# Mixture-of-experts block: the last five expert tiles on one set of sums, the other set loaded meanwhile

## The chip, the cores and the metric

One core of a Trainium2 chip runs the whole program in one launch. The metric is device time in microseconds (us) from start to end, as the median of several runs. A profile of one further run shows every instruction with its engine, its start and its length. The engines are TensorE (PE in the profile; its weight loads are PEld), VectorE (DVE), ScalarE (ACT), GpSimd (POOL) and SyncE (SP). SP issues most transfers; POOL issues the indirect ones. Sixteen DMA engines move the data.

## The reference, cut to what matters

An attention layer is followed by a layer of 16 experts, and each of the two is added to its input and normalised. The second half is what the change concerns:

```python
x = _layernorm(x + attention(x))               # 4 x 1024 tokens of 256 numbers
raw_gate = softmax(einsum('btd,de->bte', x, gate))
_, topk_idx = top_k(raw_gate, 3)               # three experts for a token
gate_topk = normalised(mask * raw_gate)
hidden = relu(einsum('btd,edh->bteh', x, W1) + b1)
expert_out = einsum('bteh,ehd->bted', hidden, W2) + b2
x = _layernorm(x + einsum('bte,bted->btd', gate_topk, expert_out))
```

All numbers are 32-bit floats.

## The kernel before

**Up to the experts.** Attention comes first; its last matmuls with the values (L479) start at 1120.7 us, the first of the experts at 1129.0 us. A router then chooses three experts for each token and writes the token's row, with its number and its gates, to a table in DRAM (`xs`), sorted by expert. Two arrays in DRAM, `sums[0]` and `sums[1]`, collect the output, one row of 256 numbers for each of the 4096 tokens. Before the experts run, `sums[0]` receives the tokens themselves (the residual) and `sums[1]` zeros.

**The tiles of the experts.** The function `moe` works through 56 tiles, t = 0 to 55 (`NUSUAL` is 56), and through some more in a branch (`tc.If`) that this input doesn't take. A full tile has 256 rows of one expert, a short one 128. In the last 32 tiles, three full ones are followed by one short one, so 51 and 55 are short and 52, 53 and 54 are full. A tile passes these steps:

- `load`: SP fetches the rows and the expert's weights (about 1.15 MB), four tiles ahead;
- `turn`: TensorE transposes the rows, VectorE copies them out (`xg`) and derives row numbers (`ids`) and gates;
- `hidden`: 16 matmuls, then four relus on ScalarE (`hid`, L1099);
- `expert_out`: 16 matmuls (8 for a short tile), then VectorE adds the bias (`y`, L1115), multiplies by the gates, one instruction for each 128 rows (L1121), and POOL issues one scatter for each 128 rows (L1125).

A scatter is an indirect DMA that adds 128 rows of 1 KB to rows of one of the two arrays of sums. The two scatters of a full tile are declared independent of each other, since a token occurs once in an expert's list; for those of different tiles nothing is declared. The set is chosen by the tile's parity (`sums_of`, L1010), so neighbours add to different sets. POOL's scatters are kept in program order (`behind`, L1014).

The orders of TensorE and SP are written out by hand in `run` (L1185). In turn t it has `turn(t+1)`, `hidden(t)`, `expert_out(t-1)`, but at the last turn `expert_out(54)` comes ahead of `hidden(55)`.

**The end.** After the tiles, `fetch` (L1217) loads both sets in nine pieces on SP's queue, `res` from `sums[0]` and `more` from `sums[1]`: seven pieces of four rows of 256 numbers for each of 128 partitions (512 KB from each set), and two pieces of two rows (256 KB). For each piece, `statistics` adds `more` to `res` on POOL (L1226), takes mean and variance on VectorE (L1230, L1232) and a root on ScalarE (L1234). `scale`, one piece behind, takes a reciprocal (L1241) and an offset (L1243) on VectorE, scales on ScalarE (L1245) and stores on SP (L1249). The orders of VectorE, ScalarE and SP are those of the program here.

Of the kernel before, what the change touches and what calls it, by code (L numbers as in the profile page):

```python
# [29 lines left out]
FP = mybir.dt.float32  # L30
# [5 lines left out]
SYNC = mybir.DependencyInfo(mybir.DependencyClass.Sync, mybir.DependencyReason.DATA)  # L36
NO_SYNC = mybir.DependencyInfo(mybir.DependencyClass.NoSync, mybir.DependencyReason.DATA)

P = 128
B, T, D = 4, 1024, 256  # L40
# [8 lines left out]
FC = FF // P  # L49
NTC = NT // P  # L50
# [16 lines left out]
NUSUAL = NL1 + NL2 + NHUSUAL  # L67
# [904 lines left out]
def moe(tc, router, first, late_rows, last_norm, acc, ident, eps_t, wall, xs, sums, out):  # L972
    nc = tc.nc
    with ExitStack() as ctx:
        def pool(name, bufs, **kw):
            return ctx.enter_context(
                tc.tile_pool(name=name, bufs=bufs, reuse_waits="tile", **kw)
            )
# [7 lines left out]
        op = pool("m_out", 1)  # L986
# [4 lines left out]
        ps_r = pool("ps_r", 1, space=PSUM)  # L991

        wall_v = wall.rearrange("(e p) r -> e p r", p=P)
        st = {}
        lists = [first, None, None, None]
        order = [(0, i) for i in range(NL0)] + [(1, i) for i in range(NL1 - NL0)]
        n_first = NL2 - 3 * NHUSUAL
# [5 lines left out]
        def of(t):  # L1003
            k, i = order[t]
            return lists[k], i

        def halves(t):
            return 1 if order[t][0] == 3 else SH

        def sums_of(t):  # L1010

            return sums[t % 2]

        def behind(i):  # L1014

            tc.add_manual_dep(i.ins, router.behind.ins.name, NO_SYNC, reason="issue order")
            router.behind = i
            return i
# [33 lines left out]
        def turn(t):  # L1052
            (_, _, rank), i = of(t)
            x, nh = st[t][0], halves(t)
            ps = ps_t.tile([P, DC, S], FP, tag="t")
            for c in range(DC):
                for h in range(nh):
                    nc.tensor.transpose(ps[:, c, ts(h, P)], x[:, h, ts(c, P)], ident)  # L1058
            xg = xgp.tile([P, DC, S], FP, tag="xg")
            with in_turn(t < NUSUAL):  # L1060
                st["turned"] = nc.vector.tensor_copy(xg[:, :, : nh * P], ps[:, :, : nh * P])  # L1061
            with tc.issue_after(st["turned"].ins):
                small(t, xg, ps)

        def in_turn(usual=True):
            return tc.issue_after(router.on_dve.ins) if usual else nullcontext()

        def small(t, xg, ps):
            (_, _, rank), i = of(t)
            x, nh = st[t][0], halves(t)  # L1070
            ids = gp.tile([P, SH], I32, tag="ids", name="ids")
            nc.vector.tensor_copy(ids[:, :nh], x[:, :nh, ID])
            mine = gp.tile([P, SH, TOPK], FP, tag="mine", name="mine")
            nc.vector.tensor_scalar(
                mine[:, :nh], x[:, :nh, RK : RK + TOPK], rank[:, i : i + 1], 1.0,
                ALU.is_equal, ALU.mult,
            )
            nc.vector.tensor_tensor(
                mine[:, :nh], mine[:, :nh], x[:, :nh, GT : GT + TOPK], ALU.mult
            )  # L1080
            gates = gp.tile([P, SH], FP, tag="gates", name="gates")
            nc.vector.tensor_reduce(gates[:, :nh], mine[:, :nh], AX.X, ALU.add)
            st[t] += [xg, ids, gates]

        def hidden(t):
            _, w, xg, _, _ = st[t]
            n = halves(t) * P
            hid = hp.tile([P, FC, S], FP, tag="hid")
            per = 512 // n
            for f0 in range(0, FC, per):  # L1090
                ps = ps_h.tile([P, per, n], FP, tag="h")
                for f in range(f0, f0 + per):
                    for c in range(DC):
                        nc.tensor.matmul(  # L1094
                            ps[:, f - f0, :], lhsT=w[:, ds(c * FF + f * P, P)], rhs=xg[:, c, :n],
                            start=(c == 0), stop=(c == DC - 1),
                        )
                for f in range(f0, f0 + per):
                    nc.scalar.activation(  # L1099
                        hid[:, f, :n], ps[:, f - f0, :], AF.Relu, bias=w[:, ds(B1_AT + f, 1)]  # L1100
                    )
            st[t].append(hid)

        def expert_out(t):
            _, w, _, ids, gates, hid = st.pop(t)
            nh = halves(t)
            ps = ps_o.tile([P, SH, D], FP, tag="o")
            for h in range(nh):
                for f in range(FC):
                    nc.tensor.matmul(  # L1110
                        ps[:, h, :], lhsT=hid[:, f, ts(h, P)], rhs=w[:, ds(W2_AT + f * D, D)],
                        start=(f == 0), stop=(f == FC - 1),
                    )
            y = yp.tile([P, SH, D], FP, tag="y")
            nc.vector.tensor_tensor(  # L1115
                y[:, :nh], ps[:, :nh],
                w[:, ds(B2_AT, D)].unsqueeze(1).to_broadcast([P, nh, D]), ALU.add,
            )
            before = None
            for h in range(nh):  # L1120
                router.on_dve = nc.vector.tensor_scalar(  # L1121
                    y[:, h, :], y[:, h, :], gates[:, h : h + 1], 1.0, ALU.mult, ALU.mult
                )
            for h in range(nh):
                s = behind(nc.gpsimd.indirect_dma_start(  # L1125
                    out=sums_of(t), out_offset=bass.IndirectOffsetOnAxis(ap=ids[:, h : h + 1], axis=0),
                    in_=y[:, h, :], in_offset=None, compute_op=ALU.add,
                ))
                if before is not None:
                    tc.declare_no_dep(  # L1130
                        s.ins, before.ins, reason="an expert has a token once: other rows"
                    )
                before = s
                if late_rows:
                    rows_of_last_but_one(3)
                elif spread_rows and t >= 5:
                    spread_rows.pop(0)()
# [15 lines left out]
        def rows_of_last_but_one(k, wait=False):  # L1153
            for _ in range(min(k, len(late_rows))):
                i = late_rows.pop(0)()
                if wait:
                    tc.add_manual_dep(
                        i.ins, st["turned"].ins.name, SYNC, reason="apart from the rows before"
                    )
# [19 lines left out]

        sums_v = [s[:NT].rearrange("(p c) d -> p c d", p=P) for s in sums]  # L1180
        out_v = out.rearrange("b t d -> (b t) d").rearrange("(p c) d -> p c d", p=P)
        rows = [(c, 4) for c in range(0, NTC - 4, 4)] + [(NTC - 4, 2), (NTC - 2, 2)]
        n_k = len(rows)

        def run(t0, t1, begun=lambda: None):  # L1185
            with tc.manual_schedule(engines={mybir.EngineType.PE, mybir.EngineType.SP}):
                for t in range(t0, t0 + 4):
                    load(t)
                turn(t0)
                begun()  # L1190
                for t in range(t0, t1):
                    if t + 4 < t1:
                        load(t + 4)
                    if t + 1 < t1:
                        turn(t + 1)
                    if t == t1 - 1:
                        expert_out(t - 1)
                    hidden(t)

                    for go in side.get(t, []):  # L1200
                        go()
                    if t0 < t < t1 - 1:
                        expert_out(t - 1)
                expert_out(t1 - 1)
# [3 lines left out]


        run(0, NUSUAL, lambda: last_norm(sp))  # L1210
        used = nc.values_load(router.used[0:1, 0:1], min_val=0, max_val=NHALF)
        with tc.If(used > NHUSUAL):
            run(NUSUAL, len(order))

        res, more = [], []

        def fetch(k):  # L1217
            c, m = rows[k]
            for of_set, got, name in ((0, res, "res"), (1, more, "more")):
                t = op.tile([P, m, D], FP, tag=f"{name}{k}", name=name)  # L1220
                nc.sync.dma_start(out=t, in_=sums_v[of_set][:, ds(c, m), :])
                got.append(t)

        def statistics(k):
            r, m = res[k], rows[k][1]
# [26 lines left out]
        with tc.manual_schedule(engines={ENG.DVE, ENG.Activation, ENG.SP}):  # L1252
            for k in range(n_k):
                fetch(k)
            for k in range(n_k):
                statistics(k)
                if k > 0:
                    scale(k - 1)
            scale(n_k - 1)
# [112 lines left out]
```

## Time and profile before

| | us |
|---|---|
| median of three runs | 1561.87 |
| lowest and highest run | 1559.64, 1563.41 |
| the profiled execution | 1561.28 |
| its span, first to last instruction | 1559.5 |
| mean granted TensorE clock, share of full | 0.985 |
| TensorE matmul busy | 1499.4 (96%) |
| last matmul ends | about 1518.5 |
| first load of the end is issued | 1523.36 |
| first add of the end | 1528.80 |

Times inside the run are us from the start of the span. A timeline row gives the start, the length, the engine, the line of the kernel, the operation, what it writes and reads, the shape and the count; a bracket tells how long the engine had been idle and what ended that. "issue" there means that the profile shows no other instruction as the cause. SPq marks what SP only hands to the DMA engines. A landing is the time from the start of an instruction that issues a DMA to the last byte's arrival.

### The profile page before, as it was taken

The page shows a single profiled execution, that of the slowest core. Times are in us where ns is not written, and L with a number is a line of the kernel's source. Part 1 is how long each engine was busy: PE and PEld are TensorE (multiplying, and loading weights), DVE is VectorE, ACT ScalarE, POOL GpSimd, SP SyncE. Part 2 cuts the span into 40 slices and gives each one's busy share as a digit, 9 for nine tenths or more (in the row PEclk, how much of TensorE's full clock was granted, in tenths as well). Part 3 has the DMA queues.
Part 4 walks back from the last instruction along what each step waited for, and adds up shares of the span by engine and source line. Part 5 has one row for each costly group of instructions (what it writes and reads, how often), then busy time and mean ns, then how long its engine had stood idle before and what let it go on. Part 6 is the DMA issues. An engine that isn't in the chain of part 4 may idle for free.

```text
span 1559.5 us, 52512 instructions
## 1 busy us (share of the span) xinstructions
PE 1499.4 (96%) x20844; PEld 1049.4 (67%) x20844; DVE 1174.7 (75%) x3679; ACT 729.6 (47%) x1693; POOL 979.6 (63%) x932
## 2 busy tenths in 40 slices
PE   8999999999999999999999999999899999999990
PEld 5566666666666666666666666665688888888880
DVE  5788888898899999878999999889857333333335
ACT  4555555557455555665555556645342222222224
POOL 3676565776556567776776667767457764444445
PEclk9999999999999999999999999999999999999995
DMA  6464545545454554564556445645488998888858
GB/s 203 128 166 123 142 117 150 152 134 176 116 143 116 149 152 119 151 191 136 150 145 171 117 129 139 192 125 137 160 311 266 373 297 226 257 257 259 258 130 329
DMA packets 120473, 280.34 MB, mean 180 GB/s; under 512 B 21392, under 2 KB 64656, under 8 KB 108688
## 3 DMA queue, kind: packets, MB, share of 16 engines
q1 hardware_dynamic: 100304, 250.05, 53.0%
q0 software_dynamic: 19584, 26.62, 8.1%
q8 instruction: 166, 2.72, 0.7%
q14 instruction: 83, 0.68, 0.1%
q10 hardware_dynamic: 336, 0.27, 0.1%
HBM read 186.81 MB, written 61.09 MB: 159 GB/s over the span
## 4 chain that ended last, share of the span: by engine, by line
PE 88%; DVE 7%; issue 2%; DMA 2%; ACT 1%; POOL 0%; SPq 0%; ACTq 0%; DVEq 0%; POOLq 0%
PE y_ps L479 18%; PE s L393 17%; PE pp L290 14%; PE ps L1110 11%; PE ps L1094 11%; PE oo L508 8%; PE vv L343 7%; PE ps L1058 1%; DVE p L401 1%; DVE t_first L452 1%; PE lg_ps L727 1%; DMA vr<-v_d 1%; DVE o_stats L1230 1%; PE x_ps L719 0%; DVE t_last L452 0%
## 5 line engine op out<-in xcount | busy, mean ns | idle before, releaser
L433 POOL TENSOR_SCALAR p<-p,rinv 128x512 f32<-128x512 f32 (+7 forms) x512 | 374.7, 747 | 336.1 <-DVE rinv L430 307.2
L416 ACT ACTIVATE p<-p,nmax 128x512 f32<-128x512 f32 (+7 forms) x512 | 391.7, 766 | 407.3 <-DVE nmax L401 318.8
L393 PE MATMUL s<-rotk,rotq 64*128 64x512 f32 (+3 forms) x1536 | 310.9, 513 | 3.3 <-DVE rotk L326 1.6
L452 DVE STREAM_TRANSPOSE t_first<-p 128x512 f32<-128x512 f32 (+3 forms) x512 | 275.8, 581 | 7.4 <-PE y_ps L479 7.3
L1125 POOL DMA_INDIRECT sums<-y,ids x104 | 163.1, 1568 | 162.2 <-DVE y L1121 128.7
L290 PE MATMUL pp<-xT,wqk 128*128 128x512 f32 x512 | 249.9, 612 | 3.4 <-DVE nmax L401 3.3
L1099 ACT ACTIVATE hid<-ps,w 128x256 f32<-128x256 f32 (+1 forms) x224 | 89.6, 455 | 289.9 <-issue 237.7
L479 PE MATMUL y_ps<-t_first,vr 32*64 32x224 f32 (+3 forms) x8192 | 206.2, 332 | 5.6 <-DVE t_first L452 2.2
L393 PEld LDWEIGHTS s<-rotk,rotq 64*128 64x128 f32 x1536 | 138.7, 186 | 100.1 <-issue 53.2
L479 PEld LDWEIGHTS y_ps<-t_first,vr 32*64 32x64 f32 x8192 | 166.9, 132 | 53.7 <-issue 45.9
L1115 DVE TENSOR_TENSOR y<-ps,w 128x512 f32<-128x512 f32 (+1 forms) x56 | 36.5, 652 | 216.7 <-PE ps L1110 184.9
L1094 PE MATMUL ps<-xg,w 128*128 128x256 f32 (+1 forms) x896 | 189.5, 365 | 1.4 <-DVE xg L1061 0.7
L1110 PE MATMUL ps<-w,hid 128*128 128x256 f32 x832 | 188.8, 379 | 0.5 <-ACT hid L1099 0.5
L401 DVE CUSTOM_DVE_ANT_0 p<-s,zero_and_mask,nmax 128x512 f32<-128x512 f32 x256 | 181.7, 747 | 2.9 <-PE s L393 0.7
L401 DVE CUSTOM_DVE_ANT_0 p<-s,mask 128x512 f32<-128x512 f32 (+1 forms) x256 | 131.8, 551 | 60.3 <-PE s L393 59.9
L1110 PEld LDWEIGHTS ps<-w,hid 128*128 128x128 f32 x832 | 157.2, 190 | 21.5 <-ACT hid L1099 0.7
L1094 PEld LDWEIGHTS ps<-xg,w 128*128 128x128 f32 x896 | 157.3, 190 | 19.1 <-DVE xg L1061 1.0
L290 PEld LDWEIGHTS pp<-xT,wqk 128*128 128x128 f32 x512 | 89.5, 189 | 119.7 <-issue 62.4
L479 PEld LDWEIGHTS y_ps<-t_last,vr 32*64 32x64 f32 x7424 | 105.2, 131 | 76.5 <-issue 49.8
L508 PE MATMUL oo<-wo,yT 128*128 128x256 f32 x512 | 141.0, 398 | 2.3 <-DVE yT L495 1.1
L479 PE MATMUL y_ps<-t_last,vr 32*64 32x32 f32 (+3 forms) x7424 | 127.1, 243 | 0.5 <-DVE t_last L452 0.4
L824 POOL DMA_INDIRECT xs<-acc,slots x96 | 97.3, 1013 | 44.0 <-issue 21.5
(191 smaller groups left out, 1835.1 us busy)
## 6 DMA issues: line engine op xcount, KB each, us to landing
w<-in_wall_dram SPq DMA_DIRECT2D x56, 1154.0 KB
vr<-v_d SPq DMA_DIRECT2D x256, 128.0 KB
vr<-v_d SPq DMA_DIRECT2D x128, 256.0 KB
swq<-rawq SPq DMA_DIRECT2D x256, 64.0 KB
v_d<-v SPq DMA_DIRECT2D x128, 128.0 KB
swk<-rawk SPq DMA_DIRECT2D x124, 128.0 KB
x<-xs SPq DMA_DIRECT2D x48, 264.0 KB
wqk<-in_w_qk_dram SPq DMA_DIRECT2D x32, 256.0 KB
```

The lines of the kernel that those rows point to most:

```text
L290: nc.tensor.matmul(ps, lhsT=wqk[n][:, c, i, :], rhs=xts[b, g][:, c, :], start=(c == 0), stop=(c == DC - 1),)
L343: nc.tensor.matmul(ps[:, u, :], lhsT=xts[b, cc // 2][:, c, ts(cc % 2 * 2 + u, P)], rhs=wv[n][:, c, :], start=(c == 0), stop=(c == DC - 1),)
L393: nc.tensor.matmul(s[:, :n_k], lhsT=rot[n, 0, qc // 4][ts(hh, KD), ts(qc % 4, P)], rhs=k[ts(hh, KD), ds(k0, n_k)], start=True, stop=True,)
L401: i = nc.vector.tensor_tensor_reduce(out=probs[n, qc, hh][:, ds(k0, n_k)], in0=s[:, :n_k], in1=masks[qc % 2][:, 512 - n_k :] if diag else ...
L416: order["exp"] = nc.scalar.activation(pr, pr, AF.Exp, bias=m, scale=-1.0, accum_out=rsum[:, hh : hh + 1])
L433: order["divide"] = router.behind = nc.gpsimd.tensor_scalar(pr, pr, rinv[:, hh : hh + 1], 1.0, ALU.mult, ALU.mult)
L452: order["turn"] = router.on_dve = after(nc.vector.transpose(turned[n][h][:, hh, :, ds(i - 4 * h, n_j, step=7 - 4 * h), :], probs[n, i, hh] ...
L479: nc.tensor.matmul(st[n][a][ts(hh, KD), ds(32 * (j + skip), 32 * (TC - j - skip))], lhsT=v[ts(a, 32), c * 8 + 2 * u + jh % 2, ts(hh, KD)], ...
L508: nc.tensor.matmul(ps[:, v, :], lhsT=st[n][:, ts(2 * h + v, P)], rhs=wo[n], start=True, stop=True,)
L1094: nc.tensor.matmul(ps[:, f - f0, :], lhsT=w[:, ds(c * FF + f * P, P)], rhs=xg[:, c, :n], start=(c == 0), stop=(c == DC - 1),)
L1110: nc.tensor.matmul(ps[:, h, :], lhsT=hid[:, f, ts(h, P)], rhs=w[:, ds(W2_AT + f * D, D)], start=(f == 0), stop=(f == FC - 1),)
L1125: s = behind(nc.gpsimd.indirect_dma_start(out=sums_of(t), out_offset=bass.IndirectOffsetOnAxis(ap=ids[:, h : h + 1], axis=0), in_=y[:, h, ...
```

## The change

- Tiles 51 to 55 all add to `sums[1]`.
- While tiles 53 to 55 run, SP loads all of `sums[0]` into `res`. These loads, `first_sums`, are now ten, the first piece being split into two of two rows, and most wait for a mark: a certain relu, bias addition or gate multiplication of a tile.
- The last two turns are written out in `last_two` (z is 55): tile 55 passes `hidden` ahead of tile 54, and `expert_out` too.
- After the tiles only `more` is loaded, in the same ten pieces.
- In the branch that isn't taken here, `res` is loaded again at the end.

```diff
         def sums_of(t):
-            return sums[t % 2]
+            return sums[1 if NUSUAL - 5 <= t < NUSUAL else t % 2]
...
-                    nc.scalar.activation(
+                    marks["hid", t, f] = nc.scalar.activation(
...
-            nc.vector.tensor_tensor(
+            marks["y", t] = nc.vector.tensor_tensor(
...
+            marks["scaled", t] = router.on_dve
...
-        rows = [(c, 4) for c in range(0, NTC - 4, 4)] + [(NTC - 4, 2), (NTC - 2, 2)]
+        rows = [(0, 2), (2, 2)] + [(c, 4) for c in range(4, NTC - 4, 4)] + [(NTC - 4, 2), (NTC - 2, 2)]
         n_k = len(rows)
+        res = [op.tile([P, m, D], FP, tag=f"res{k}", name="res") for k, (_, m) in enumerate(rows)]
+
+        def first_sums(k, *mark):
+            c, m = rows[k]
+            d = nc.sync.dma_start(out=res[k], in_=sums_v[0][:, ds(c, m), :])
+            if mark:
+                tc.add_manual_dep(d.ins, marks[mark].ins.name, SYNC, reason="one after another")
+
+        def last_two(z):
+            first_sums(0, "hid", z - 2, FC - 1)
+            first_sums(1)
+            first_sums(2, "y", z - 3)
+            turn(z)
+            first_sums(3, "scaled", z - 3)
+            expert_out(z - 2)
+            first_sums(4, "y", z - 2)
+            first_sums(5, "scaled", z - 2)
+            hidden(z)
+            first_sums(6, "hid", z, FC - 1)
+            hidden(z - 1)
+            first_sums(7, "hid", z - 1, FC // 2 - 1)
+            first_sums(8, "hid", z - 1, FC - 1)
+            first_sums(9)
+            expert_out(z)
+            expert_out(z - 1)
...
                 for t in range(t0, t1):
+                    if t == NUSUAL - 2:
+                        last_two(t + 1)
+                        return
                     if t + 4 < t1:
...
             run(NUSUAL, len(order))
-        res, more = [], []
+            for k in range(n_k):
+                first_sums(k)
+
+        more = []
 
         def fetch(k):
             c, m = rows[k]
-            for of_set, got, name in ((0, res, "res"), (1, more, "more")):
-                t = op.tile([P, m, D], FP, tag=f"{name}{k}", name=name)
-                nc.sync.dma_start(out=t, in_=sums_v[of_set][:, ds(c, m), :])
-                got.append(t)
+            t = op.tile([P, m, D], FP, tag=f"more{k}", name="more")
+            nc.sync.dma_start(out=t, in_=sums_v[1][:, ds(c, m), :])
+            more.append(t)
```

More of the change, by code (lines that the diff above doesn't have):

```diff
@@ L993, in moe @@
         wall_v = wall.rearrange("(e p) r -> e p r", p=P)
-        st = {}
+        st, marks = {}, {}
         lists = [first, None, None, None]
```

## The prediction

> **What bounds the kernel now.** I read four views in this order: the chain of waits from 1440 us on, the timeline of GpSimd (POOL) around the last tiles, the timelines after 1523 us, and the landing times of scatters, by windows that hold one or a few. t numbers the tiles, 0 to 55; the short last one is 55. E is the time at which the last scatter has landed.
>
> The chain of waits (start, duration, what):
>
> ```profile
> 1507.30 6.92 PE ps L1110 x32
> ...
> 1515.86 1.55 POOL sums L1125
> ...
> 1517.72 5.57 DMA sums<-y,ids
> ...
> 1524.87 6.70 DMA more<-sums
> ```
>
> TensorE is the chain up to 1514.2 us. After that it is the scatters, then the first loads of the two sets, then the last norm. The change touches only the end, so the sum is made there.
>
> The scatters of t=52 (second half), 53 (second half), 54 and 55, from the POOL timeline:
>
> ```profile
> 1506.88 1.55 POOL L1125 DMA_INDIRECT sums<-y,ids  x1 [0.30 <-issue]
> ...
> 1514.01 1.55 POOL L1125 DMA_INDIRECT sums<-y,ids  x1 [0.30 <-issue]
> ...
> 1517.72 1.55 POOL L1125 DMA_INDIRECT sums<-y,ids  x1 [0.30 <-issue]
> 1519.64 1.55 POOL L1125 DMA_INDIRECT sums<-y,ids  x1 [0.36 <-DVE y L1121]
> ```
>
> Each in a window of its own, they land 3.6, 3.7, 3.9 and 3.9 us after these starts. So E = 1519.64 + 3.9 = 1523.5. In 1442 to 1500 us, with weight loads in flight, the median is 6.8 us:
>
> ```profile
> DMA to landing us min/median/max: 3.8/6.8/7.7
> ```
>
> Does a scatter wait for the one before it on the same set? The code forgoes that order only for the two halves of one tile (`declare_no_dep`, L1130). The trace shows such a wait near 1262 us:
>
> ```profile
> 1257.92 1.56 POOL L1125 DMA_INDIRECT sums<-y,ids  x1 [0.30 <-DVE y L1115]
> 1262.63 1.55 POOL L1125 DMA_INDIRECT sums<-y,ids  x1 [3.15 <-issue]
> ```
>
> POOL stands idle for 3.15 us. The scatter of 1252.87 took 9.0 us by its own window and landed at 1261.9; the next started 0.7 us later. I take that 0.7 as the step from a landing to the next scatter. Today the two sets alternate, so near the end each scatter finds its set free: all seven after 1500 us start behind DVE or behind POOL itself.
>
> The last norm (POOL adds, VectorE statistics and offsets):
>
> ```profile
> 1523.36 0.33 SPq L1221 DMA_DIRECT2D res<-sums  x1
> 1523.83 0.53 SPq L1221 DMA_DIRECT2D more<-sums  x1
> ...
> 1528.80 2.34 POOL L1226 TENSOR_TENSOR res<-res,more 128x1024 f32<-128x1024 f32 x1 [7.60 <-DMA more<-sums]
> ...
> 1542.18 2.35 POOL L1226 TENSOR_TENSOR res<-res,more 128x1024 f32<-128x1024 f32 x1 [0.21 <-DMA more<-sums]
> ...
> 1543.78 0.76 DVE L1243 SCALAR_TENSOR_TENSOR o_off<-o_mv,o_rstd 128x4 f32<-128x4 f32 x1
> ...
> 1544.75 4.80 POOL L1226 TENSOR_TENSOR res<-res,more 128x1024 f32<-128x1024 f32 x3 [0.22 <-DMA more<-sums]
> ...
> 1550.54 0.16 DVE L1243 SCALAR_TENSOR_TENSOR o_off<-o_mv,o_rstd 128x4 f32<-128x4 f32 x1
> ```
>
> VectorE looks full here (4.9 of every 5 us), but the pace is not its own. Its offset ends where POOL's add ends (1543.78 + 0.76 = 1544.54; 1542.18 + 2.35 = 1544.53) and takes 0.16 us once POOL is done. POOL waits for `more` before each of its adds up to 1544.75. The pace is that of the loads: about 2.55 us for 1 MB of the two sets. Where both are there, the adds follow at once: 4.80 us for a 4-row and two 2-row adds, so 2.30 and 1.25.
>
> **The change part by part.** The profiled execution took 1561.28 us (span 1559.5, 1.8 around it), 0.6 under the median of the runs.
>
> *The new order on TensorE.* `expert_out(53)`, `hidden(55)`, `hidden(54)`, `expert_out(55)`, `expert_out(54)` in place of `hidden(54)`, `expert_out(53)`, `expert_out(54)`, `hidden(55)`, `expert_out(55)`. They are the same 72 matmuls; the wait for the relus of tile 55 (0.51 us) goes, since `hidden(54)`, 3.5 us, lies between. y of 53 is added at about 1507.3 instead of 1510.8, y of 55 about 1514.4, and TensorE ends near 1517.8 instead of 1518.5. ScalarE's four relus for 55 (1.1 us) and two pairs for 54 lie beside matmuls. None of this is late enough to set E, as the next part shows.
>
> *Five tiles on set 1.* Tiles 52 and 54 move there. Now 53 waits for 52, 55 for 53, 54 for 55. Without loads beside them:
> - the second half of 52 starts at 1506.88 as before (51 landed at 1497.41 + 3.8) and lands at 1510.5;
> - 53 starts at 1511.2 (+0.7), its second half 1.86 later at 1513.1, landed 1516.8 (+3.7);
> - 55 starts at 1517.5 (its y is ready by 1515.4), landed 1521.3 (+3.8);
> - 54 starts at 1522.0 (ready by 1519.2), second half 1523.9, landed 1527.8 (+3.9).
>
> So E moves by +4.3 us. Nothing is queued on POOL behind these waits but the next scatter and the adds of the norm; the norm's loads of set 1 wait for the last landing. The order of 54 and 55 does not alter the sum of this row of waits.
>
> Here a rule speaks against my price. The Trainium skill, "DMA: Bandwidth & Descriptors", "Anatomy of one DMA — SWDGE (gpsimd) path", fits such a DMA as about 2.0 us plus bytes over 436 GB/s, which is 2.3 us for 128 KB. By it tile 54 would go out when its y is ready, E would move by 1.4 us, and the sum below would be -2.8; no scatter above landed that soon.
>
> *Set 0 loaded meanwhile.* Ten loads, 4.2 MB, on SP's queue, with the waits on ScalarE's and VectorE's marks. Set 0's last scatter (t=50, 1493.91) lands by 1501.6 even at 7.7 us, and all weight loads were issued by 1491.5, so nothing waits on SP behind these marks but the branch of the `If`, which SP passed at 1492 and will reach near 1514, well ahead of E. Ten issues of 0.3 to 0.5 us are hidden there. What is not hidden is the delay to scatters. Loads of the norm moved 1531 packets in 14 us at a share of 101%:
>
> ```profile
> q1 hardware_dynamic: 1531, 5.56, 101.1%
> ```
>
> That is 14 x 16 / 1358 full packets (the same view has 173 under 512 B) = 0.16 us each. A scatter has 128 rows, 8 an engine; if each lets one packet pass, it lands 1.3 us later. By the marks, the load behind y of 53 (issued about 1508.1) meets the second half of 52, whose data pass near 1509 to 1510; the second half of 53 (data after 1515) meets little, as the last loads leave SP near 1514. Bounds: 0, and 3.2 for each of the two (6.8 against 3.6, the weight loads' row). I take 1.3, the packets' own size being known. E: +4.3 + 1.3 = +5.6 us.
>
> On the same point the skill's page, "Queues, rings and completion order", says an engine drains a packet of some 9 to 17 descriptors before it switches rings. At the page's 27 GiB/s an engine, with 4 KB descriptors, an estimate by it is 1.3 to 2.4 us for one such turn, so which would make the sum +1.4 to +2.5; no row here shows the turns.
>
> *The end.* The first add needs 256 KB in place of two loads of 512 KB: 5.3 us from E to 1528.80, less 1.9 (0.75 MB at 1 MB in 2.55 us), less 0.4 (one issue ahead of it is gone): 3.0. Then the adds run without waiting, for half the bytes arrive: 6 x 2.30 + 4 x 1.25 = 18.8, so the last ends at E + 21.8. Before it ended at 1549.54, E + 26.0. What follows (two 2-row blocks on VectorE, ScalarE's scaling, the last store) is the same in both. Saved: 4.2 us. The extra 2-row block costs VectorE about 1 us of work that lies under the adds. Bounds: 2.7 if the 4-row adds stay at 2.55 (1.5 less), 4.6 if the first load takes 2.6.
>
> Sum: +5.6 - 4.2 = +1.4 us: 1562.7 against the profiled execution, 1563.3 against the median. This is likeliest; its own range is 1561.6 (no load term, 4.6 saved) to 1564.8 (load term 2.4, 3.8 saved). A measurement of this kernel can tell about 0.2%, 3.1 us, from no change, so this counts as no change.
>
> **The rivals.**
> - *No wait between tiles of one set.* Then E is set by y of 54: scatters at 1519.2 and 1521.0, landed 1524.9, E + 1.4, and the sum is -2.8: 1559.1. For: the waits name a landing as the releaser of a scatter for 0.3 us at most. Against: the 3.15 us above.
> - *Slower: the loads hold the scatters up as weight loads do.* Landings at 6.8 us cost 3.2 for 52 alone, 6.3 with 53. The sum is +3.3 to +6.4, middle 1566.8. It decides from a load term of 3.0 on. For: 17 scatters with that median. Against: weight loads have rows of 9 KB, these 4 KB at most, and SP spreads them out.
> - *The adds do not quicken.* VectorE's offset and POOL's add exclude each other; if POOL yields each time, the pace stays 2.55 and 2.7 are saved: +2.9, 1564.8. Against: at 1547.05 POOL went on while an offset was waiting.
>
> That the set 0 loads come late and save nothing would need a mark after 1517; the latest is the relu of 54, about 1513.5.
>
> **How the numbers follow.** Forecast 0.52 (same 0.45, slower 0.06, faster 0.01); no wait 0.16 (faster 0.09, same 0.07); loads hold up 0.17 (slower 0.16, same 0.01); adds not quicker 0.15 (same 0.08, slower 0.07). So faster 0.10, same 0.61, slower 0.29. The range, 1559.1 to 1566.8, reaches from the first rival to the middle of the second; about 0.17 is left out.
>
> **What would show it.** Right: POOL idle for over 2 us before the scatters of 53, 55 and 54, released by landings; the last start near 1525.2 and E near 1529; the first add 3 us after; 4-row adds every 2.3 us. Wrong: scatters that start right behind VectorE (first rival), landings over 5.5 us for 52 or 53 (second), adds 2.55 apart (third).

## The result and the profile after

The changed kernel takes 1566.24 us (median of 21 runs, 1563.70 to 1569.63) against 1561.65 us for the kernel before (21 runs, 1558.75 to 1564.61). The ratio is 1.0028, with a 95% interval of 1.0021 to 1.0035. That is slower, by somewhat more than the 0.2% that counts as a difference here. The profiled execution of the changed kernel took 1566.24 us (span 1564.5), against 1561.28 (span 1559.5).

The two kernels are the same up to the last tiles. So all times below are counted from T, the start of the first scatter of tile 52: 1505.02 us before, 1505.50 after. From T to the end of the span it is 54.5 us before and 59.0 after, which makes +4.5 of the +5.0; the other 0.5 lies ahead of T.

The timeline of GpSimd (start, duration, ..., idle time before it and what ended it) shows the scatters of 52, 53, 55 and 54 and then the adds of the norm:

```profile
1505.50 1.55 POOL L1126 DMA_INDIRECT sums<-y,ids  x1 [6.06 <-DVE y L1121]
1507.36 1.55 POOL L1126 DMA_INDIRECT sums<-y,ids  x1 [0.30 <-issue]
1514.47 1.55 POOL L1126 DMA_INDIRECT sums<-y,ids  x1 [5.56 <-DMA sums<-y,ids]
1516.33 1.55 POOL L1126 DMA_INDIRECT sums<-y,ids  x1 [0.30 <-issue]
1521.24 1.55 POOL L1126 DMA_INDIRECT sums<-y,ids  x1 [3.35 <-DMA sums<-y,ids]
1525.65 1.55 POOL L1126 DMA_INDIRECT sums<-y,ids  x1 [2.86 <-issue]
1527.51 1.55 POOL L1126 DMA_INDIRECT sums<-y,ids  x1 [0.30 <-issue]
1534.04 2.48 POOL L1256 TENSOR_TENSOR res<-res,more 128x512 f32<-128x512 f32 x2 [4.98 <-DMA more<-sums]
1538.36 16.30 POOL L1256 TENSOR_TENSOR res<-res,more 128x1024 f32<-128x1024 f32 x8 [1.84 <-DMA more<-sums]
```

Before 53, 55 and 54 POOL now stands idle for 5.56, 3.35 and 2.86 us, and the first two idle times end with the landing of an earlier scatter. The third is put down to "issue", but it is the same wait: 55 lands 3.7 us after 1521.24, that is at 1524.9, and 54 starts 0.7 us later, the step from a landing to the next start that the kernel before shows near 1262 us.

The chain of waits (start, duration, what) is followed back to the scatter of 55 and no further:

```profile
1521.24 1.55 DMA sums<-y,ids
...
1527.51 3.75 DMA sums<-y,ids
...
1532.18 6.11 DMA more<-sums
...
1538.36 2.35 POOL res L1256
```

The scatter of 55 is now a link of it, where before it held one of 54 alone. E, when the last scatter has landed, is 1527.51 + 3.75 = 1531.26. The first add starts 2.8 us after E. The 6.11 us under `more<-sums` are the loads that the third add waits for; after that add, nothing waits for a load, and the norm runs at POOL's pace.

### The profile page after: what moved, and what is told of

Same layout as the page of the kernel before. It is cut to its first block, busy times and chain, and to the rows that moved or that the text cites. A ratio compares the mean times of both kernels' runs of the same rounds, so it can differ in the third digit from the quotient of the medians.

```text
span 1564.5 us, 52524 instructions
## 1 busy us (share of the span) xinstructions
PE 1499.1 (96%) x20844; PEld 1048.2 (67%) x20844; DVE 1173.2 (75%) x3681; ACT 730.6 (47%) x1694; POOL 980.2 (63%) x933
```

## The experiments

The experiments ran on three chips on which the kernel before takes 1580 to 1582 us: sets_alone to three_tiles of the table on one, changed_again to order_alone on the next, the last two on the third. So their times are compared as ratios to the runs of the kernel before that stand beside them, with 95% intervals, and their traces from T. Each has one trace, and the kernel before has none on these chips. Two traces of the changed kernel itself (after and changed_again) differ by 0.6 us in E, so a difference of that size between two rows says nothing. This table holds the readings from the traces; "52 lands" is counted from the start of the second half's scatter of 52, all else from T, in us:

| kernel | 52 lands | 53 starts | 55 starts | 54 starts | E | last add ends | ratio of the times |
|---|---|---|---|---|---|---|---|
| before | 3.6 | 7.13 | 14.62 | 10.84 | 18.5 | 44.5 | 1 |
| after | 6.4 | 8.97 | 15.74 | 20.15 | 25.8 | 49.2 | 1.0028 (1.0021 to 1.0035) |
| sets_alone | 3.9 | 7.13 | 20.11 | 13.45 | 24.0 | 50.9 | 1.0044 (1.0027 to 1.0062) |
| sets_and_order | 3.8 | 6.39 | 13.42 | 17.91 | 23.5 | 50.6 | 1.0049 (1.0032 to 1.0066) |
| two_tiles_unscattered | none | 3.67 | none | 14.09 | 19.6 | 44.1 | 1.0000 (0.9982 to 1.0017) |
| three_tiles | 3.7 | 3.78 | 10.38 | 17.03 | 23.0 | 47.4 | 1.0008 (0.9987 to 1.0028) |
| changed_again | 6.4 | 9.00 | 16.15 | 20.72 | 26.4 | 49.6 | 1.0026 (1.0011 to 1.0041) |
| three_at_a_time | 6.4 | 8.96 | 16.77 | 21.18 | 26.8 | 48.8 | 1.0015 (1.0001 to 1.0030) |
| set_0_read_twice | 6.3 | 8.84 | 15.93 | 20.40 | 25.9 | 50.2 | 1.0031 (1.0017 to 1.0045) |
| order_alone | 3.8 | 3.78 | 10.37 | 14.09 | 19.8 | 46.0 | 0.9991 (0.9973 to 1.0009) |
| loads_behind_52 | 4.1 | 6.73 | 18.14 | 22.71 | 28.3 | 52.0 | 1.0031 (1.0017 to 1.0044) |
| three_tiles_apart | 3.8 | 3.78 | 10.37 | 14.88 | 23.0 | 48.3 | 1.0015 (0.9999 to 1.0030) |

In two_tiles_unscattered, T is put 7.61 us behind the start of 51's scatter, where the other kernels have it.

### The parts of the change, one at a time

**sets_alone**: the last five tiles on one set, with the loads and the order of the kernel before.

```
-            return sums[t % 2]
+            return sums[1 if NUSUAL - 5 <= t < NUSUAL else t % 2]
```

> The kernel before with one line changed: tiles 51 to 55 all add to set 1; order of the tiles and loads of the end as before. If the waits between tiles of one set are the cost: the scatters of 54 start near 1518.5 (the second half of 53 lands at 1517.7, and 0.7 to the next start), those of 55 near 1524.9, the last lands near 1528.8 in place of 1523.5, and the time is 5.2 us above before. If the loads beside the tiles are the whole cost: no difference from before.

E moves by 5.4 us and the time by 0.44%. Tile 54 waits for the landing of 53, as POOL's timeline has it:

```profile
1534.87 1.55 POOL L1125 DMA_INDIRECT sums<-y,ids  x1 [2.90 <-DMA sums<-y,ids]
```

53 itself doesn't wait: in the old order its y is ready only at T + 7.13, after 52 has landed. 55 waits in the same way for 54. The wait between tiles of one set is real, and it costs time by itself.

**sets_and_order**: the changed kernel, with set 0 loaded beside set 1 after the last scatter.

```
         def last_two(z):
-            first_sums(0, "hid", z - 2, FC - 1)
... (and the other calls of first_sums)
         def fetch(k):
             c, m = rows[k]
+            first_sums(k)
             t = op.tile([P, m, D], FP, tag=f"more{k}", name="more")
```

> The changed kernel without its early loads: five tiles on set 1, the short tile ahead, but both sets loaded at the end, in pairs of the ten pieces. If the waits are the cost: no landing slower than 4 us after 1500, the last scatter lands 4.3 us later than before, and the time is 3.5 to 4.5 us above before, about that of the changed kernel. If the loads beside the scatters are the whole cost: within 1 us of before.

All three tiles wait for a landing:

```profile
1526.19 1.55 POOL L1126 DMA_INDIRECT sums<-y,ids  x1 [2.98 <-DMA sums<-y,ids]
...
1533.22 1.55 POOL L1126 DMA_INDIRECT sums<-y,ids  x1 [3.62 <-DMA sums<-y,ids]
1537.71 1.55 POOL L1126 DMA_INDIRECT sums<-y,ids  x1 [2.94 <-issue]
```

E moves by 5.0 us; with no load beside the scatters, that is the price of the waits. Set against the changed kernel (E + 7.3), the early loads cost 2.3 us of E. In the three other traces that have the same early loads (set_0_read_twice, changed_again, three_at_a_time) it is 2.5, 2.9 and 3.3 us. The time moved more than was expected, by 0.49%, some 5 to 10 us in place of 3.5 to 4.5: the last add ends 6.1 us later than before, 1.1 more than E accounts for.

**order_alone**: the kernel before with the new order of TensorE's work.

```
+        def last_two(z):
+            turn(z)
+            expert_out(z - 2)
+            hidden(z)
+            hidden(z - 1)
+            expert_out(z)
+            expert_out(z - 1)
```

> The kernel before with the new order of the last tiles on TensorE and nothing else: sets by parity, loads of both at the end. By the sum: 53 goes out 3.4 us sooner, but y of 54 comes last, so its scatters start at 14.2 and 16.0 us after the first of 52 and land at 19.9, 1.4 us later than before; the time is 1.4 us above before. If the order is what brings the loss: 3 us or more above.

With the sets alternating, each scatter starts behind VectorE again, 53 already at T + 3.78:

```profile
1525.23 1.55 POOL L1125 DMA_INDIRECT sums<-y,ids  x1 [0.36 <-DVE y L1121]
...
1531.82 1.55 POOL L1125 DMA_INDIRECT sums<-y,ids  x1 [3.18 <-DVE y L1121]
1535.54 1.55 POOL L1125 DMA_INDIRECT sums<-y,ids  x1 [2.17 <-DVE y L1121]
```

E moves by 1.3 us, since the longer tile is now last. In time it isn't told from no change (0.9991, 0.9973 to 1.0009). So the waits in the other kernels come from the shared set, not from the order.

### What the early loads do to the scatters

**two_tiles_unscattered**: the changed kernel without the scatters of 52 and 55.

```
-            for h in range(nh):
+            for h in range(0 if t in (NUSUAL - 4, NUSUAL - 1) else nh):
```

> The changed kernel, but tiles 52 and 55 are computed and not scattered (their share of the sums is left out), so that 53 finds its set free and 54 has only 53 ahead of it. The early loads stay. If the waits are the cost: 53 goes out at 1508.7, 54 at 1519.2, the last landing is 1.4 us later than before, and with 2.6 us saved behind it the time is about 1.2 us below before (0 to 3 below). If the loads beside the scatters are the whole cost: 1 us or more above before, as 53 and 54 still pass beside them.

With half of the row of waits gone, E is 1.1 us later than before, as expected, and the time is that of the kernel before (1.0000) and not 1.2 us below it. The first half of 53 now goes out while the loads run, and its second half lands 7.8 us after its start; 54, with nothing beside it, takes 3.7. The last add ends 24.5 us after E, against 26.0 before.

**three_tiles**: only 53, 54 and 55 share set 1. Three pieces of set 0 are handed to SP behind the scatter of 53, two behind that of 55, and the rest among the loads after E.

```
-            return sums[1 if NUSUAL - 5 <= t < NUSUAL else t % 2]
+            return sums[1 if NUSUAL - 3 <= t < NUSUAL else t % 2]
...
+            first_sums(0, "scatter", z - 2)
+            first_sums(1)
+            first_sums(2)
...
             expert_out(z)
+            first_sums(3, "scatter", z)
+            first_sums(4)
             expert_out(z - 1)
```

> A version of the change: only the tiles 53 to 55 add to set 1 (52 goes to set 0), so the wait of 53 for 52 is gone; five of the ten loads of set 0 run early, three after the landing of 53 and two after that of 55, the others in between the loads of set 1 at the end. By the waits: 53 at 1508.7, landed 1514.3; 55 at 1515.4, landed 1519.2; 54 at 1519.9, landed 1525.7, 2.2 us later than before; behind it 2.6 to 4.2 us are saved, so the time is 0.4 to 2.0 us below before. If loads near a scatter cost about 3 us wherever they are: 1 us or more above before.

52 and 53 go out as in order_alone. But the loads behind 53 meet 55, which lands after 5.9 us, so 54 starts at T + 17.0 and not at 14.9:

```profile
1534.53 1.55 POOL L1126 DMA_INDIRECT sums<-y,ids  x1 [3.19 <-DVE y L1121]
1541.18 1.55 POOL L1126 DMA_INDIRECT sums<-y,ids  x1 [5.10 <-issue]
```

E is 4.5 us later than before, where 2.2 was expected. The time isn't told from that of before (1.0008, 0.9987 to 1.0028).

**three_tiles_apart**: the same with the third piece moved behind 55.

```
             first_sums(1)
-            first_sums(2)
...
-            first_sums(3, "scatter", z)
+            first_sums(2, "scatter", z)
+            first_sums(3)
             first_sums(4)
```

> Three tiles on set 1 as before in these experiments, but only two loads of 256 KB run after the landing of 53 and the next three after that of 55, so that the scatter of 55 passes alone. If loads beside a scatter delay it: 55 lands in 3.7 to 4.2 us (5.9 with one load more ahead of it), the last landing is 2.4 to 3.5 us later than before in place of 4.5, and the time is from 1 us below to 1 us above before. If not: 55 takes 5 us or more and the time is 1 us or more above before.

Now 55 lands after 3.8 us and 54 starts at T + 14.9, 0.7 us after that landing, though the row names another releaser:

```profile
1532.54 1.55 POOL L1126 DMA_INDIRECT sums<-y,ids  x1 [3.18 <-DVE y L1121]
1537.05 1.55 POOL L1126 DMA_INDIRECT sums<-y,ids  x1 [2.95 <-DVEq L1236]
```

But the three loads behind 55 meet 54, whose halves land 7.5 and 6.2 us after their starts. E is where it was, T + 23.0, and not 1 to 2 us sooner as expected.

**loads_behind_52**: the changed kernel, with the fifth piece and all behind it held until 52 has landed.

```
-            first_sums(4, "y", z - 2)
+            first_sums(4, "scatter", z - 3)
```

> The changed kernel, but the fifth load of set 0, and with it all behind it on SP, waits until the second half of 52 has landed in place of y of 53. If a load in flight beside a scatter is what delays its landing: 52 lands under 4.5 us after its start (6.4 in the changed kernel), the second half of 53 now passes beside the loads and takes 5.5 us or more (4.2 to 4.6), so the wait moves from one link to the next and the time stays within 2 us of the changed kernel. If 52 is slow for another reason (its wait, the new order): it still takes over 6 us.

52 lands after 4.1 us in place of 6.4, and 53 starts 2.2 us earlier than in the changed kernel. Then 53's halves take 9.4 and 8.8 us:

```profile
1530.51 1.55 POOL L1126 DMA_INDIRECT sums<-y,ids  x1 [3.32 <-DMA sums<-y,ids]
1532.37 1.59 POOL L1126 DMA_INDIRECT sums<-y,ids  x1 [0.30 <-issue]
1541.92 1.56 POOL L1126 DMA_INDIRECT sums<-y,ids  x1 [7.96 <-DMA sums<-y,ids]
```

E ends up 2.5 us later still. Wherever 1 MB of loads or more was put beside a scatter, that tile paid; the 0.5 MB ahead of 55 in three_tiles_apart cost it nothing.

How it pays is seen in the packets of the two DMA queues (packets, MB, share of 16 engines; q0 carries the scatters, q1 the loads). In sets_and_order, the two scatters of 52 have the DMA engines to themselves from 1521.6 to 1525.5, 1.8 to 5.7 us after T. They are 288 packets, 144 for each scatter:

```profile
q0 software_dynamic: 288, 0.26, 59.3%
```

Read in steps of 0.5 us, the packets of each start 2.1 us after the start of its instruction and are through in about 1.4 us. In the changed kernel, the second half of 52 is due at 1507.36 + 2.1 = 1509.5 and lands by 1513.7. From 1509.5 to 1513.2:

```profile
q1 hardware_dynamic: 215, 0.82, 67.0%
q0 software_dynamic: 183, 0.16, 29.7%
```

Beside what was left of the first half and the whole second half, 215 packets of the loads went through: 13.4 on each engine in the mean, 2.1 us at the prediction's 0.16 us each, and 2.5 us by the view's own share (67.0% of 3.7 us). And in loads_behind_52, from 1532.6, when the first half of 53 is due, to 1535.5 the view has the loads alone:

```profile
q1 hardware_dynamic: 308, 1.11, 102.1%
```

That is 19 on each engine between the time when the scatter's packets were due and the first of them. From 1529.7 to 1535.5 the loads moved 1.61 MB. SP had handed out four of 512 KB from 1529.8 to 1531.2, 2.1 MB, and two of 256 KB at 1532.2 and 1532.6. three_tiles_apart has the same picture: 54's packets are due at 1539.1 and start at 1541.7, when 1.33 of the 1.57 MB handed out ahead of them have moved. So of the loads handed out 1.4 us or more before a scatter's packets were due, about four fifths went ahead of them in these two kernels. Those handed out less than 1 us before, at 1508.5 and 1509.3 in the changed kernel, ran beside the packets of 52's second half.

### The end

**changed_again**: the changed kernel itself on the chip of the two that follow.

> The changed kernel itself, beside the others of this group on one chip. Both theories: 0.2% to 0.4% above before; the second half of 52 lands 5 us or more after its start, the last landing is some 7 us later than before counted from the start of the first scatter of 52, and the third add waits 1.5 us or more for its load of set 1.

```profile
1555.94 2.48 POOL L1256 TENSOR_TENSOR res<-res,more 128x512 f32<-128x512 f32 x2 [5.28 <-DMA more<-sums]
1559.76 16.32 POOL L1256 TENSOR_TENSOR res<-res,more 128x1024 f32<-128x1024 f32 x8 [1.34 <-DMA more<-sums]
```

The ratio is 1.0026, close to the 1.0028 of the first pair, and the pattern from T is the same within 0.6 us. The third add waits 1.34 us, the last add ends 23.2 us after E.

**three_at_a_time**: at most three loads of set 1 under way.

```
+            d = nc.sync.dma_start(out=t, in_=sums_v[1][:, ds(c, m), :])
+            if k > 2:
+                tc.add_manual_dep(d.ins, issued[k - 3].ins.name, SYNC, reason="three at a time")
+            issued.append(d)
```

> The changed kernel, but from the fourth load of set 1 on each waits until the load three before it has landed, so that SP does not hand out ten in a row. If the handing out of many loads in a row is what slows the loads of set 1 (some 270 KB in a us in place of 410): about 400 KB in a us from the second us on, the third add waits under 0.3 us, and the time is 1.5 to 1.8 us below the changed kernel. If the first reads of these rows are slow however they are handed out: the rate stays under 330, the wait of 1.5 us or more stays, and the time is the same or more.

```profile
1556.57 2.48 POOL L1259 TENSOR_TENSOR res<-res,more 128x512 f32<-128x512 f32 x2 [5.21 <-DMA more<-sums]
1559.28 16.32 POOL L1259 TENSOR_TENSOR res<-res,more 128x1024 f32<-128x1024 f32 x8 [0.23 <-DMA more<-sums]
```

The third add no longer waits (0.23 us), and the last one ends 22.1 us after E, 1.1 us sooner than in changed_again. In all other traces whose end is that of the changed kernel or nearly so, the third add waits 1.3 to 2.7 us. The loads moved 352 GB/s from 3 to 7 us after E, against 267 in changed_again, and not the 400 that was expected. By time the two aren't told apart: 1.0015 (1.0001 to 1.0030) and 1.0026 (1.0011 to 1.0041).

**set_0_read_twice**: the loads after E read set 0, which has long been complete, so set 1 is left out of the result.

```
-            nc.sync.dma_start(out=t, in_=sums_v[1][:, ds(c, m), :])
+            d = nc.sync.dma_start(out=t, in_=sums_v[0][:, ds(c, m), :])
+            tc.add_manual_dep(d.ins, last_scatter[0].ins.name, SYNC, reason="as late as the other set")
```

> The changed kernel, but the loads after the last landing read set 0 a second time in place of set 1 (so set 1 is left out of the result), at the same point of time. If rows just written by scatters are slow to read: about 400 KB in a us and no wait at the third add, 1.5 to 1.8 us below the changed kernel. If the handing out, or any first few us of loads, is slow: no difference, under 330 KB in a us.

```profile
1553.79 2.48 POOL L1258 TENSOR_TENSOR res<-res,more 128x512 f32<-128x512 f32 x2 [5.26 <-DMA more<-sums]
1558.58 16.30 POOL L1258 TENSOR_TENSOR res<-res,more 128x1024 f32<-128x1024 f32 x8 [2.31 <-DMA more<-sums]
```

The third add waits 2.31 us, longer than in changed_again. The loads move 303 GB/s from 3 to 7 us after E. So that the rows were written just before isn't what makes the first loads slow.

## Why the prediction was right or wrong

The prediction's sum was +4.3 + 1.3 - 4.2 = +1.4 us. By the traces it is +5.0 (sets_and_order) + 2.3 (the changed kernel against sets_and_order) - 2.8 (the part behind E) = +4.5. The time lies inside the range (1559.1 to 1566.8), near its upper end, and outside the likeliest case's own range (up to 1564.8). The forecast of "no change within 0.2%" failed; slower had 0.29. Each of the three terms was too low or too hopeful, by 0.7, 1.0 and 1.4 us, all the same way.

**The waits between tiles: right in kind, 0.7 us short.** POOL stands idle before 53, 55 and 54, and a landing starts the next scatter 0.7 us later, as said. Without loads, sets_and_order starts 53, 55 and 54 at T + 6.4, 13.4 and 17.9, where the prediction has 6.2, 12.5 and 17.0. The difference comes in mostly at one place: 53's second half took 4.4 us there, against 3.7 in the kernel before. That may be the spread of single traces, as the same scatter took 3.7 us in sets_alone. The first rival, no wait between tiles of one set, falls: order_alone has no such wait and sets_alone has it. What it would have left of E, +1.4 for the order, is what order_alone shows (+1.3).

On this point the Trainium skill, "DMA: Bandwidth & Descriptors", "Anatomy of one DMA — SWDGE (gpsimd) path", would make a scatter of 128 KB 2.3 us, an estimate from its fit. In every run with nothing beside it, it took 3.6 to 4.4 us. The measurement decides.

**The loads beside the scatters: the step that failed most clearly.** "Each lets one packet pass" was a count of 8 load packets on each DMA engine for one scatter. 13.4 went through beside the second half of 52. By the count these are 2.1 us, by the view's share 2.5, and so most or nearly all of the 2.6 us by which 52 landed later than in sets_and_order (6.4 against 3.8). What is left would be the first half, which started its packets about 1 us late behind the loads handed out at 1504.9 and 1505.5; in loads_behind_52, where that alone is left, it costs 52 0.3 us. The prediction named the load behind y of 53 as the one that meets the second half. The trace has another at 1509.3, also before the scatter's packets were due. That 53's second half meets little was right in this trace: it took 4.2 us, against 4.4 without loads (4.5 to 5.2 in the three others with the same early loads). The first half of 53, which the prediction did not price, took 5.4 us against 3.7, but landed 0.6 us ahead of the second.

This was the second rival's mechanism, and its sign came true: 52 landed later than the 5.5 us set as its mark. Whether its price did is not settled: the term is 2.3 in the profiled execution and 2.5 to 3.3 in the other three traces, around the 3.0 from which it was to decide. The result is near its middle (1566.8) also because the other two terms fell short. loads_behind_52 shows a larger price still: there the scatters of 53 took 9.4 and 8.8 us.

The skill's section "Queues, rings and completion order" on the same page says that an engine drains a packet of some 9 to 17 descriptors of one ring before it switches. If a packet of the profile is a descriptor of the page, the 13.4 beside 52 agree; the 19 ahead of 53 in loads_behind_52 are a little more. By that rule the load term was an estimated 1.3 to 2.4. The 2.3 lies there and the 2.9 and 3.3 lie above it, so the rule was nearer than the row that was chosen.

**The end: right in three of four numbers.** The first add starts 2.8 us after E (3.0 said). The adds by themselves take 2.48 + 16.30 = 18.8 us, to the tenth what was said, and the 4-row adds follow each other every 2.3 us. So the third rival falls too. VectorE's offset still ends with POOL's add, but POOL doesn't yield; from the timeline of the changed kernel, beside an add and after the last one:

```profile
1544.81 0.51 DVE L1273 SCALAR_TENSOR_TENSOR o_off<-o_mv,o_rstd 128x4 f32<-128x4 f32 x1
...
1555.66 0.16 DVE L1273 SCALAR_TENSOR_TENSOR o_off<-o_mv,o_rstd 128x4 f32<-128x4 f32 x1
```

What failed is "then the adds run without waiting, for half the bytes arrive". The third add waited 1.84 us. The first loads after E came slowly, as the windows of the changed kernel show (length, busy time of PE, PEld, DVE, ACT and POOL, clock, DMA share, GB/s):

```profile
1534.30:1538.30 4.00, 0.00 (x0) 0.00 (x0) 2.15 (x10) 1.02 (x3) 2.22 (x2) 0.50 0.86 261
1538.30:1542.30 4.00, 0.00 (x0) 0.00 (x0) 1.57 (x8) 0.66 (x2) 3.94 (x2) 0.50 1.01 394
```

The prediction took the pace of the kernel before, 1 MB in 2.55 us, from the first load on. The slower pace is only a part of the wait, though. The third add needs three loads, 1.05 MB, and by 1536.5, when POOL had done the first two adds, 1.14 MB had gone through. But some of that belonged to later loads. The trace counts the landing of a load in sixteen steps: of the third load's, thirteen had come by 1536.95 and the last came at 1538.29, when 1.63 MB had moved. two_tiles_unscattered, where the third add waits 2.53 us, is alike: fourteen steps by 1551.45, the last at 1554.19. So the saving up to the last add was 2.6 us, not 4.2.

In the one trace of three_at_a_time, where fewer loads are handed out at once, the wait is gone. Why the first loads are slow stays open. set_0_read_twice excludes the fresh rows as the cause. That many loads are under way isn't enough as a cause: order_alone hands out as many in a row, and from 3 to 7 us after E they move 417 GB/s. Nor are the two small pieces at the front the cause, for sets_alone has none and moves 265:

```profile
1546.00:1552.00 6.00, 0.00 (x0) 0.00 (x0) 0.00 (x0) 0.00 (x0) 0.00 (x0) 0.50 0.82 261
1552.00:1556.00 4.00, 0.00 (x0) 0.00 (x0) 1.44 (x6) 0.00 (x0) 3.60 (x2) 0.50 1.02 412
```

What the traces have in common is this: from 3 to 7 us after E, the nine kernels that end with several tiles on one set and hand out all loads at once move 262 to 331 GB/s, the two that alternate to the end 362 (before) and 417 (order_alone). No run tells why.

No kernel was measurably faster than the one before. The row of waits costs 5.0 us of E with five tiles on one set, and the saving behind E was 2.8.

## What to carry to other kernels

Before loads are put "beside" other DMAs, list for each of those when its packets are due, and count every load that is handed out well before that moment: about four fifths of their bytes went ahead in two kernels here, at about 1.3 us for 512 KB (half of the 2.55 us for 1 MB). Scatters to one array that aren't declared independent ran one after another, so alternating two destinations was worth more here than having one of them complete early. And a pace read from the middle of a burst of loads needn't hold for its first megabyte, which is the part that the next engine waits for.

## What had not been expected of the hardware

- The delay of a scatter went with how much of the loads had been handed out and not moved yet when its packets came due, some 2 us behind its start: with 0.5 MB handed out up to 0.4 us before 55's scatter it took 3.8 us (three_tiles_apart); with 2 MB, 53's second half took 8.8 us (loads_behind_52).
- A scatter of 128 rows of 1 KB spends 2.1 us before its first packet, about 1.4 us with packets, and the rest of its 3.6 to 3.9 us before it counts as landed. Loads ahead of it make the first packet late (by about 1 us for 52 in the changed kernel, by 2.9 us for 53 in loads_behind_52), and loads beside it stretch the packets (the second half of 52 had packets until 1513.2, 3.7 us after they were due).
- From 3 to 7 us after E the loads of the changed kernel moved 261 GB/s, with no other DMA beside them, where the same queue moved 394 GB/s in the next 4 us. The last three of the sixteen steps in which a load's landing is counted came 1.1 to 1.3 us after the first thirteen, and it was these that the third add waited for.
